# A planned emission order with other costs, one reduction for layer 0's sixteen terms, and a third row-mask buffer in a four-layer graph kernel

## The chip, the core and the metric

The kernel runs on one core of one Trainium2 chip. A core has a matrix engine (TensorE, "PE" in the profile, with its weight load "PEld"), a vector engine (VectorE, "DVE"), a scalar engine (ScalarE, "ACT"), GpSimd ("POOL"), which here only issues transfers, and SyncE ("SP"), which issues the others. Each engine takes its instructions in the order in which the program emitted them, and semaphores let one engine wait for another. The metric is the device time of one launch in microseconds (us), the median of several runs.

## The reference, cut to what matters

There are N = 2048 nodes, a batch of B = 8 and C = 64 features. Each of four layers adds a graph operation to x and normalizes the result over the 64 features.

```
x = layernorm(x + L0(x, adj))
#   L0: As = [I, A, 2*A@A - I];  out[b,n,o] = sum_k sum_i (As[k] @ x)[b,n,i] * w[n,k,i,o] + bias[n,o]
#       w = einsum('nd,dkio->nkio', embedding, weight), d = 16 terms for each node
x = layernorm(x + L1(x, adj))
#   L1: e = leaky_relu(s1[:, :, None] + s2[:, None, :]);  att = softmax(where(adj > 0.5, e, -9e15))
#       elu(att @ x)
x = layernorm(x + L2(x, adj))
#   L2: ((adj + I) @ (x @ W.T + b)) / rowsum(adj + I)
x = layernorm(x + L3(x, adj))
#   L3: three steps of  effects = adj @ v;  v = relu([v, effects] @ W1.T + b1) @ W2.T + b2
```

All data are float32.

## The kernel before, in words

**Tiles.** The eight batches are handled as four pairs (p = 0 to 3); a pair's 2 x 64 features fill 128 columns. `SX[p]` holds the pair's x as 16 tiles of 128 nodes. A product with the adjacency (a "sweep") walks over four column chunks of 512 nodes (c) and eight tiles of 256 x 512 elements (q), which `fetch` loads through SP's queue into a ring of `A_BUFS` buffers of 512 KB (tile `a`). The matmuls of a sweep stand in `sweep` at L1086; they accumulate in PSUM tiles `acc`.

**Layer 0.** `second_pass` (matmuls at L593) makes for each tile of 128 nodes two PSUM tiles `yp`, each with eight of the 16 embedding terms. `add_terms` weights each term with the node's embedding and adds it to `SX`. It has three forms: for most tiles ScalarE writes 16 weighted terms into an `e` buffer (L616) and VectorE adds them pairwise (L630, L632); for pair 0 ScalarE takes the first eight and VectorE adds the others straight to `SX` (L618); and where the plan sees no free `e` buffer, VectorE does all 16. `first_norm` and `layer_norm` (L471 to L498) follow.

**Layer 1.** Row masks (`mr`, L431) are made once from the rows of adj in `row_tile`, and stored in DRAM (`by_row`); column masks (`mk`, L447) likewise (`by_col`). `scores` finds the greatest score of each row: 16 row tiles, each with one mask load (L712) and two VectorE instructions (L724, tile `junk`). `weights` then makes the exponentials column tile by column tile: mask load (L797), VectorE add (L802), ScalarE Prelu (L810), VectorE add (L815), ScalarE Exp (L818), and eight matmuls for two column tiles (L828, tile `po`). Four `e` buffers serve this chain and layer 0's terms. `finish` divides, applies the ELU and normalizes.

**Layers 2 and 3.** After a sweep, `z_evict` or `h_evict` (L946) take the PSUM tile to SBUF, and `tails` runs the small products of a chunk: `ps_emb` (L974), VectorE (L983, L987), the norm, `ps_vT` (transpose, L1008), `ps_u` (L1021), `ps_v` (L1041). Pairs 0 and 1 are done one after the other; pairs 2 and 3 together at the end in `joint_layer2` (L1205) and `joint_layer3` (L1292), which work on sums of quarters of adj that `sums` makes on VectorE (L1165) and stores in DRAM.

**What sets the order.** The program is emitted by a planner. Each piece of work is a Python generator (a "thread") that yields the engine of its next step and the things it waits for. `Plan.go` keeps an estimated time at which each engine is free, picks the thread whose next step could begin earliest, and lets it emit its instructions; `plan.run` advances the engine's estimated time by a cost written in the code. A step on PE counts as ready only `SLACK` us after its inputs are. `Ring` is a set of buffers with estimated times of release. All this happens while the program is built; on the chip only the resulting order per engine and the semaphores remain.

Of the kernel before, what the change touches and what calls it, by code (L numbers as in the profile page):

```python
# [37 lines left out]
class Plan:  # L38
# [6 lines left out]
    SLACK = 2.5  # L45

    def __init__(self):
        self.free = dict.fromkeys(["PE", "DVE", "ACT", "DMA", "SP"], 0.0)
        self.at = {}
        self.threads = []  # L50
        self.count = itertools.count()
# [8 lines left out]
    def run(self, eng, cost, *after):  # L60
        t = max([self.free[eng], *(self.when(a) for a in after)]) + cost
        assert t < NEVER
        self.free[eng] = t
        return t + self.LAG

# [70 lines left out]
def resnorm_d4_kernel(  # L136
# [44 lines left out]
    mr_ring = Ring(wp, "mr", 2)  # L181
# [36 lines left out]
    A_BUFS = 7  # L218
# [7 lines left out]
    def fetch(n):  # L226
        c, q, plus = order_of_a[n]
        t, k = a_ring.take([P, 2, CW], "a")
        freed = a_ring.t
        if isinstance(c, str):  # L230
            src = sum_tiles[c][q]
        else:
            src = a_plus_i[q] if plus and c == q // 2 else tile_of_adj(c, q)
        nc.sync.dma_start(t, src)
        a_tiles[n] = (t, k)
        at["a", n] = plan.run("SP", 1.4, freed) + 3.5
# [23 lines left out]
    blocks = ("w2bd", "w31v", "w31e", "w32bd", "w32c")  # L260
    w2bd, w31v, w31e, w32bd, w32c = (const.tile([P, P], F32, name=n) for n in blocks)
# [107 lines left out]
    def weights_of_l23():  # L369
# [20 lines left out]
        pp_ring.give(k, done)  # L390
        yield "PE", [pp_ring, done]
# [19 lines left out]
    def rows_of_adj():  # L411


        for t in range(NT):
            yield "SP", [115.0 + 9.0 * t, bc_ring]
            an, k = bc_ring.take([P, 2, HALF], "an")
            an = an.rearrange("p a b -> p (a b)")
            nc.sync.dma_start(an, adj[t * P : (t + 1) * P, :])
            done = plan.run("SP", 2.8, bc_ring.t, 115.0 + 9.0 * t) + 9.0
            plan.start(1, row_tile(t, an, k, done))  # L420

    def row_tile(t, an, k, done):
        yield "ACT", [done]
        dg = tiny([P, 1], "dg", 2)
        nc.scalar.activation(an, an, AF.Copy, accum_out=dg)
        done = plan.run("ACT", act(N) + 0.2, done)
        yield "DVE", [done, mr_ring]
        nc.vector.tensor_scalar_add(dg, dg, 1.0)
        nc.vector.reciprocal(rdeg[:, t : t + 1], dg)
        mk, km = mr_ring.take([P, N], "mr", BF16)  # L430
        nc.vector.tensor_scalar(mk, an, THRESHOLD, NEG_INF, ALU.is_le, ALU.mult)  # L431
        done = plan.run("DVE", 1.13 + 0.16, done)
        bc_ring.give(k, done)
        nc.gpsimd.dma_start(by_row[t], mk)
        done = plan.run("DMA", 0.6, done) + 4.0
        mr_ring.give(km, done)
        at["by_row", t] = done + 2.0
        if all(("by_row", i) in at for i in range(NT)):
            at["rows"] = done

    def mask_of_tile(n, t, k):
# [7 lines left out]
        if c == q // 2:  # L449
            yield "DVE", [got]  # L450
            for i in range(2):
                block = t[:, i, (2 * q + i) % TPC * P :][:, 0:P]
                nc.vector.tensor_tensor(block, block, ident, ALU.add)
            got = plan.run("DVE", dve(P, 2), got)
            nc.gpsimd.dma_start(a_plus_i[q], t)
            got = plan.run("DMA", 0.6, got) + 4.0
        a_ring.give(k, max(done, got))
        nc.gpsimd.dma_start(by_col[q][:, :, cols(c)], mk)
        done = plan.run("DMA", 0.8, done) + 4.0
        mk_ring.give(km, done)  # L460
        at["by_col", q, c] = done + 2.0

    def layer_norm(v, n, after, centered=False):
# [4 lines left out]
        if not centered:  # L468
# [7 lines left out]
            done = plan.run("DVE", dve(n, 2) + 0.1, after)  # L476
# [9 lines left out]
        done = plan.run("DVE", dve(n) + 0.1, done)  # L486
# [5 lines left out]
        done = plan.run("ACT", 0.3, done)  # L492
        yield "DVE", [done]

        nc.vector.tensor_tensor(vs, vs, r, ALU.mult)
        nc.vector.scalar_tensor_tensor(vs, vs, -0.5, r, ALU.mult, ALU.mult)
        nc.vector.scalar_tensor_tensor(r, vs, 1.5, r, ALU.add, ALU.mult)
        nc.vector.tensor_tensor(v3, v3, r.unsqueeze(2).to_broadcast([P, nb, C]), ALU.mult)  # L498
        return plan.run("DVE", dve(n) + 0.4, done)
# [7 lines left out]
    def y1_chunk(p, c, pa, ka, done):  # L507
# [6 lines left out]
        stored = plan.run("DMA", 0.6, done) + 3.0  # L514
        at["y1T", p, c] = stored + 2.0
# [23 lines left out]
    def stacks():  # L539

        for n in range(NPAIR * NCH):
# [6 lines left out]
            got = plan.run("DMA", 0.6, xg_ring.t, ("y1T", p, c)) + 4.0  # L548
# [15 lines left out]
    def second_pass():  # L564

        for n in range(NPAIR * NCH):
# [4 lines left out]
            for j in range(TPC):  # L571
                t = c * TPC + j
                cs = slice(j * P, (j + 1) * P)
                for h in range(2):
# [5 lines left out]
                    if h == 0 or ring.ready() > plan.free["PE"]:  # L580
                        yield "PE", [("xg", n + 1), got, ring]
                    if h == 0:


                        terms = None
                        if e_ring.ready() < NEVER:
                            terms = e_ring.take([P, D0, P], "terms")
# [17 lines left out]
    def add_terms(p, c, t, h, yp, ring, k, terms, t_pe, left):  # L605

        shared = p == 0 and terms is not None
        eng = "ACT" if terms and not (shared and h) else "DVE"
        yield eng, [t_pe]
        v = SX[p][:, t, :]  # L610
        for d in range(8):
# [5 lines left out]
            else:  # L617
                nc.vector.scalar_tensor_tensor(  # L618
                    batches(v), term, weight, batches(v), ALU.mult, ALU.add
                )  # L620
        done = plan.run(eng, 8 * (0.25 if eng == "ACT" else 0.265), t_pe)
# [4 lines left out]
        if terms:  # L626
            yield "DVE", [done, ("terms", p, t)]
            for half in (4, 2) if shared else (8, 4, 2):
                a, b = (terms[0][:, i * half : (i + 1) * half, :] for i in range(2))
                nc.vector.tensor_tensor(a, a, b, ALU.add)  # L630
            for d in range(2):
                nc.vector.tensor_tensor(v, v, terms[0][:, d, :], ALU.add)  # L632
            done = plan.run("DVE", 1.4 if shared else 2.5, done, ("terms", p, t))
            e_ring.give(terms[1], done)
# [59 lines left out]
    def scores(p, sv, xc, s_rows, done):  # L694
        s2b = []
        for e in range(2):
# [5 lines left out]
            ready = plan.run("DMA", 0.8, done, bc_ring.t) + 7.5  # L702
# [6 lines left out]
        def load(t):  # L709
# [4 lines left out]
            at["mask", p, t] = plan.run("DMA", 0.6, mr_ring.t, ("by_row", t)) + 5.0  # L714

        plan.start(1, load(0))
        for h in range(2):
            mx = tiny([P, 2, 8], "mx", 4)
            for t in range(8 * h, 8 * h + 8):
                if t + 1 < NT:  # L720
                    plan.start(1, load(t + 1))
# [20 lines left out]
    def greatest(p, h, mx, sv, xc, s_rows, done):  # L742
# [5 lines left out]
        done = plan.run("DVE", 0.16, done)  # L748
# [7 lines left out]
        for name, rows in (  # L756
# [7 lines left out]
            ready = plan.run("DMA", 0.8, done, bc_ring.t) + 8.0  # L764
# [7 lines left out]
    def to_rows(v, rows, done):  # L772
# [12 lines left out]
        done = plan.run("DMA", 0.5, done) + 2.5  # L785
# [5 lines left out]
    def weights(p, h, jt, s1b, mb, sv, po, ready):  # L791
# [6 lines left out]
        got = plan.run("DMA", 0.6, mk_ring.t) + 4.5  # L798
# [14 lines left out]
        done = plan.run("ACT", act(HALF, 2), done)  # L813
# [6 lines left out]
        mine = held.setdefault((p, h), [])  # L820
        mine.append((jt, e, ke, done))
        if jt % 2 == 0:
            return
        yield "PE", [mine[0][3], done, *([("weighed", p, h, jt - 2)] if jt > 1 else [])]
# [14 lines left out]
        mine.clear()  # L839
# [6 lines left out]
    def finish(p, h, po, kpo, xc):  # L846
# [11 lines left out]
        for f in range(2):  # L858
# [24 lines left out]
            done = plan.run("DVE", dve(CW) + 0.12, t_pe)  # L883
# [21 lines left out]
            done = plan.run("DVE", dve(CW, 2) + 0.2, done)  # L905
# [3 lines left out]
        if h == 0:  # L909
            yield "DMA", [("weighted", p, 1)]  # L910
            nc.gpsimd.dma_start(SX[p][:, 0:8, :], stage)
            done = plan.run("DMA", 1.5, *norms) + 3.0
# [57 lines left out]
    def layer2_tail(p, c, z, kz, done):  # L970
# [19 lines left out]
        done = plan.run("DVE", dve(P, TPC) + dve(CW), done)  # L990
# [46 lines left out]
    def last_chunk(p, c, done):  # L1037
# [15 lines left out]
        done = plan.run("DVE", dve(CW, 2), done)  # L1053
# [88 lines left out]
    def pure(k, r):  # L1142
# [3 lines left out]
        for c, q in (quarters(k, r)[i] for i in (0, 3)):  # L1146
            t, kt = xg_ring.take([P, 2, CW], "pure")
            nc.sync.dma_start(t, tile_of_adj(c, q))
            got.append((t, kt, plan.run("SP", 1.4, xg_ring.t) + 4.0))
        return got  # L1150

    def sums(k, r, taken):
# [8 lines left out]
        def out_of(m, a, b, op, *after):  # L1161
# [6 lines left out]
            bc_ring.give(kt, plan.run("DMA", 0.6, done) + 5.0)  # L1168
# [302 lines left out]
```

## Time and profile before

| what | before |
|---|---|
| median of 3 runs | 2172.77 us (2169.68 to 2172.82) |
| the profiled execution | 2177.32 us, its span 2175.5 us |
| mean granted TensorE clock | 0.984 |
| PE busy | 2090.3 us, 96% of the span |
| DVE busy | 1532.3 us, 70% |
| ACT busy | 933.5 us, 43% |
| moved by DMA | 495.85 MB, mean 228 GB/s |
| adjacency tiles, issue to landing | 496 of 512 KB, 5.3 us (median) |
| row-mask loads, issue to landing | 64 of 512 KB, 5.9 us (median) |

The span is the time from the first to the last instruction of one profiled execution; the rest of its time lies around it. "Busy" is the time in which at least one instruction of an engine ran. A line of a group reads: source line, engine, operation, output tile <- input tiles, shapes, count | busy us, mean ns of one | idle us of the engine before them and what ended it. In a table of stretches each engine's busy time is given with its instruction count, then the granted clock (1.00 is full speed), the DMA engines' busy share and the rate in GB/s. An fp32 matmul of the program is two instructions in the profile.

### The profile page before, as it was taken

How to read it: one execution, taken by the hardware profiler on the slowest of the kernel's cores; microseconds unless marked ns; L12 is line 12 of the kernel's file. 1: busy time of each engine (PE TensorE's matmuls, PEld its weight loads, DVE VectorE, ACT ScalarE, POOL GpSimd, SP SyncE). 2: the span in 40 equal slices, each digit the busy share in tenths (PEclk: the TensorE clock that was granted, in tenths of full speed). 3: DMA queues.
4: the chain of work that ended last, by engine and by line, in shares of the span. 5: the costliest groups of instructions: out<-in, count | busy, mean ns of one | idle time of the engine just before them, and what ended most of it. 6: DMA issues, size and time to landing. Idle time of an engine off the chain costs nothing. (4 is left out here: it accounts for less than half of the span.)

```text
span 2175.5 us, 19004 instructions
## 1 busy us (share of the span) xinstructions
PE 2090.3 (96%) x6325; PEld 923.0 (42%) x6325; DVE 1532.3 (70%) x2057; ACT 933.5 (43%) x1605; POOL 213.3 (10%) x374
## 2 busy tenths in 40 slices
PE   8998999999999999999998999989999998999997
PEld 3443444333433333344443444434444454444443
DVE  2226756999799999979998978989797555020214
ACT  0014433476576457767624746417566012000001
POOL 2211001100110110001001011011100110000000
PEclk9999999999999999999999999989999999999999
DMA  9798845633542475446688788778687687878785
GB/s 313 270 328 305 287 133 184 216 107 96 162 150 88 150 234 153 146 126 198 223 289 299 247 286 294 233 249 303 220 293 226 238 301 243 281 251 282 252 291 169
DMA packets 208739, 495.85 MB, mean 228 GB/s; under 512 B 20274, under 2 KB 28594, under 8 KB 204530
## 3 DMA queue, kind: packets, MB, share of 16 engines
q1 hardware_dynamic: 165058, 347.62, 48.3%
q0 software_dynamic: 39360, 144.92, 19.4%
q10 hardware_dynamic: 4224, 2.10, 0.4%
q8 instruction: 50, 0.82, 0.1%
q14 instruction: 47, 0.39, 0.1%
HBM read 446.14 MB, written 46.33 MB: 226 GB/s over the span
## 5 line engine op out<-in xcount | busy, mean ns | idle before, releaser
L1086 PE MATMUL acc<-a,SX 128*128 128x512 f32 x1024 | 470.1, 603 | 9.0 <-DMA SX<-in_x 6.4
L1086 PE MATMUL acc<-a,SA 128*128 128x512 f32 x768 | 352.9, 602 | 8.0 <-ACT SA L348 4.7
L810 ACT ACTIVATE e<-e,sv 128x1024 f32<-128x1024 f32 x256 | 280.4, 1153 | 123.6 <-DVE e L802 117.3
L724 DVE CUSTOM_DVE_ANT_0 junk<-s2b,mr 128x2048 bf16<-128x2048 f32 x128 | 292.7, 2287 | 32.6 <-DMA mr<-by_row 31.3
L818 ACT ACTIVATE e<-e 128x2048 f32<-128x2048 f32 x128 | 245.3, 1925 | 120.5 <-DVE e L815 120.2
L802 DVE TENSOR_TENSOR e<-s1b,mk 128x2048 f32<-128x2048 f32 x128 | 289.6, 2284 | 9.8 <-DMA mk<-by_col 9.8
L815 DVE TENSOR_TENSOR e<-e,mb 128x2048 f32<-128x2048 f32 x128 | 290.2, 2284 | 7.6 <-ACT e L810 7.5
L1086 PEld LDWEIGHTS acc<-a,SX 128*128 128x128 f32 x1024 | 191.7, 193 | 242.7 <-issue 229.1
L593 PE MATMUL yp<-SH,xgT 128*128 128x512 f32 x512 | 250.7, 615 | 1.8 <-DVE SX L618 1.0
L616 ACT ACTIVATE terms<-yp,emb_sb 128x128 f32<-128x128 f32 x768 | 207.9, 396 | 70.9 <-PE yp L593 70.6
L828 PE MATMUL po<-e,SX 128*64 128x512 f32 x1024 | 234.0, 599 | 3.0 <-ACT e L818 3.0
L1086 PEld LDWEIGHTS acc<-a,SA 128*128 128x128 f32 x768 | 142.6, 192 | 182.0 <-issue 168.3
L1292 PE MATMUL acc<-a,t 128*128 128x512 f32 x384 | 169.1, 592 | 0.0
L593 PEld LDWEIGHTS yp<-SH,xgT 128*128 128x128 f32 x512 | 92.4, 193 | 147.6 <-issue 139.0
L593 PE MATMUL yp<-SH,y2T 64*128 64x512 f32 x512 | 134.9, 634 | 17.3 <-ACT terms L616 9.8
L630 DVE TENSOR_TENSOR terms<-terms 128x512 f32<-128x512 f32 (+1 forms) x152 | 111.2, 731 | 35.6 <-ACT terms L616 32.2
L828 PEld LDWEIGHTS po<-e,SX 128*64 128x64 f32 x1024 | 68.0, 137 | 155.6 <-issue 137.8
L797 POOL DMA_DIRECT2D mk<-by_col x128 | 69.3, 542 | 589.4 <-DVE e L802 475.9
L618 DVE SCALAR_TENSOR_TENSOR SX<-yp,emb_sb,SX 128x128 f32<-128x128 f32 x256 | 89.7, 350 | 48.9 <-PE yp L593 40.4
L1086 PE MATMUL acc<-a,SB 128*128 128x512 f32 x256 | 120.1, 601 | 0.0
L1292 PEld LDWEIGHTS acc<-a,t 128*128 128x128 f32 x384 | 72.0, 190 | 86.1 <-issue 86.1
L480 ACT ACTIVATE ln_sq<-SX 128x512 f32<-128x512 f32 x48 | 30.4, 633 | 146.4 <-DVE SX L473 81.1
(226 smaller groups left out, 1704.2 us busy)
## 6 DMA issues: line engine op xcount, KB each, us to landing
a<-in_adj_t SPq DMA_DIRECT2D x496, 512.0 KB, 5.3
a<-s SPq DMA_DIRECT2D x96, 512.0 KB, 4.5
mr<-by_row POOLq DMA_DIRECT2D x64, 512.0 KB, 5.9
mk<-by_col POOLq DMA_DIRECT2D x128, 256.0 KB, 5.6
an<-in_adj SPq DMA_DIRECT2D x16, 1024.0 KB, 9.3
s<-s POOLq DMA_DIRECT2D x32, 512.0 KB, 6.9
a<-a_plus_i SPq DMA_DIRECT2D x24, 512.0 KB, 5.7
by_col<-mk POOLq DMA_DIRECT2D x32, 256.0 KB, 6.1
```

The source lines that it names most:

```text
L593: nc.tensor.matmul(yp[:, e, :], lhsT=y2T[rows, cs] if k2 else xg[:, e, cs], rhs=(wk2 if k2 else w01)[rows, hs], start=(k2 == h), stop=(k2 ...
L616: nc.scalar.activation(batches(terms[0][:, dd, :]), term, AF.Copy, scale=weight)
L618: nc.vector.scalar_tensor_tensor(batches(v), term, weight, batches(v), ALU.mult, ALU.add)
L630: nc.vector.tensor_tensor(a, a, b, ALU.add)
L724: nc.vector.tensor_tensor_reduce(out=junk, in0=s2b[e][0], in1=masks[t][0], scale=1.0, scalar=LOWEST, op0=ALU.add, op1=ALU.max, accum_out=m ...
L802: nc.vector.tensor_tensor(e, s1b[0], mk.unsqueeze(1).to_broadcast([P, 2, HALF]), ALU.add)
L810: nc.scalar.activation(e[:, i, :], e[:, i, :], AF.Prelu, bias=sv[:, 2 + i, jt : jt + 1], alpha=ALPHA)
L815: nc.vector.tensor_tensor(e, e, mb[0], ALU.add)
L818: nc.scalar.activation(e, e, AF.Exp)
L828: nc.tensor.matmul(po[i * C : (i + 1) * C, f, :], lhsT=SX[p][:, t, i * C : (i + 1) * C], rhs=e[:, i, f * CW : (f + 1) * CW], start=(t == 0 ...
L1086: nc.tensor.matmul(pa, lhsT=source[:, m, :], rhs=t[:, i, :], start=(m == 0 and not seed), stop=(m == NT - 1),)
L1292: nc.tensor.matmul(pa, lhsT=B[:, 2 * r + b, :], rhs=at_[:, b, :], start=(r == 0 and b == 0 and not go_on), stop=(r == RQ - 1 and b == 1), ...
```

## The change

The change has these parts. Line numbers below are those of the kernel before.

- The planner: `SLACK` goes from 2.5 to 1.0; a new method `dma` estimates a transfer's end from its size at a shared rate (`RATE` = 340, in KB per us) in place of fixed delays at each call; about a dozen costs of VectorE's and ScalarE's chains become larger, by up to 0.35 us.
- Layer 0: `add_terms` has two forms in place of three. The terms always go to an `e` buffer, for which TensorE's step now waits in the plan. For pair 0 VectorE's eight terms are added in place to ScalarE's eight. The sum of the 16 (or 8) terms is one `tensor_reduce` over an access pattern whose inner step is 128 elements, and one addition to `SX`.
- `layer_norm`: one small VectorE product (L495) is replaced by a Square on ScalarE.
- Buffers: the row-mask ring `mr` has three buffers in place of two and `scores` loads two tiles ahead; `A_BUFS` goes from 7 to 6; the weight block `w32bd` moves into the `stage` buffer; the list `held` of `weights` is keyed by column tile.

The diff, cut to its core:

```diff
-    SLACK = 2.5
+    RATE = 340.0
+    SLACK = 1.0
...
+    def dma(self, queue, kb, *after):
+        t = self.run(queue, 0.4 if queue == "SP" else 0.7, *after) - self.LAG
+        self.moved = max(t + 3.5, self.moved) + kb / self.RATE
+        return self.moved + 0.2
...
-    mr_ring = Ring(wp, "mr", 2)
+    mr_ring = Ring(wp, "mr", 3)
...
-    A_BUFS = 7
+    A_BUFS = 6
...
-        at["a", n] = plan.run("SP", 1.4, freed) + 3.5
+        at["a", n] = plan.dma("SP", 512, freed)
...
-    w2bd, w31v, w31e, w32bd, w32c = (const.tile([P, P], F32, name=n) for n in blocks)
+    w2bd, w31v, w31e, w32c = (const.tile([P, P], F32, name=n) for n in blocks)
+    w32bd_t, w32bd_k = st_ring.take([P, 8, P], "w32bd")
+    w32bd = w32bd_t[:, 0, :]
...
-        done = plan.run("DVE", 1.13 + 0.16, done)
+        done = plan.run("DVE", 1.13 + 0.26, done)
         bc_ring.give(k, done)
         nc.gpsimd.dma_start(by_row[t], mk)
-        done = plan.run("DMA", 0.6, done) + 4.0
+        done = plan.dma("DMA", 512, done)
...
         nc.scalar.activation(r, vs, AF.Ln)
         nc.scalar.activation(r, r, AF.Exp, scale=-0.5)
-        done = plan.run("ACT", 0.3, done)
+        rr = tiny([P, nb], "ln_rr", 2)
+        nc.scalar.activation(rr, r, AF.Square)
+        done = plan.run("ACT", 0.55, done)
         yield "DVE", [done]
-        nc.vector.tensor_tensor(vs, vs, r, ALU.mult)
-        nc.vector.scalar_tensor_tensor(vs, vs, -0.5, r, ALU.mult, ALU.mult)
+        nc.vector.scalar_tensor_tensor(vs, vs, -0.5, rr, ALU.mult, ALU.mult)
...
-                        yield "PE", [("xg", n + 1), got, ring]
+                        yield "PE", [("xg", n + 1), got, ring, *([e_ring] if h == 0 else [])]
                     if h == 0:
-                        terms = None
-                        if e_ring.ready() < NEVER:
-                            terms = e_ring.take([P, D0, P], "terms")
+                        terms = e_ring.take([P, D0, P], "terms")
...
-        shared = p == 0 and terms is not None
-        eng = "ACT" if terms and not (shared and h) else "DVE"
-        yield eng, [t_pe]
+        shared = p == 0
+        eng = "DVE" if shared and h else "ACT"
+        yield eng, [t_pe, *([("terms", p, t)] if shared and h else [])]
...
-                nc.vector.scalar_tensor_tensor(
-                    batches(v), term, weight, batches(v), ALU.mult, ALU.add
-                )
-        done = plan.run(eng, 8 * (0.25 if eng == "ACT" else 0.265), t_pe)
+                to = batches(terms[0][:, d, :])
+                nc.vector.scalar_tensor_tensor(to, term, weight, to, ALU.mult, ALU.add)
+        done = plan.run(eng, 8 * (0.255 if eng == "ACT" else 0.29), t_pe)
...
-            for half in (4, 2) if shared else (8, 4, 2):
-                a, b = (terms[0][:, i * half : (i + 1) * half, :] for i in range(2))
-                nc.vector.tensor_tensor(a, a, b, ALU.add)
-            for d in range(2):
-                nc.vector.tensor_tensor(v, v, terms[0][:, d, :], ALU.add)
-            done = plan.run("DVE", 1.4 if shared else 2.5, done, ("terms", p, t))
+        n = 8 if shared else D0
+        added = tiny([P, P], "added", 1)
+        nc.vector.tensor_reduce(
+            added, terms[0][:, 0:n, :].rearrange("p d n -> p n d"), AX.X, ALU.add
+        )
+        nc.vector.tensor_tensor(v, v, added, ALU.add)
+        done = plan.run("DVE", dve(n * P) + dve(P) + 0.1, done)
...
-            at["mask", p, t] = plan.run("DMA", 0.6, mr_ring.t, ("by_row", t)) + 5.0
+            at["mask", p, t] = plan.dma("DMA", 512, mr_ring.t, ("by_row", t)) + 0.5
         plan.start(1, load(0))
+        plan.start(1, load(1))
...
-                if t + 1 < NT:
-                    plan.start(1, load(t + 1))
+                if t + 2 < NT:
+                    plan.start(1, load(t + 2))
...
-        got = plan.run("DMA", 0.6, mk_ring.t) + 4.5
+        got = plan.dma("DMA", 256, mk_ring.t) + 0.3
...
-        done = plan.run("ACT", act(HALF, 2), done)
+        done = plan.run("ACT", act(HALF, 2) + 0.15, done)
...
-        done = plan.run("DVE", dve(P, TPC) + dve(CW), done)
+        done = plan.run("DVE", dve(P, TPC) + dve(CW) + 0.35, done)
```

## The prediction

> **What bounds the kernel now.** The page's first part and its table of stretches come first: they tell which engine has no idle time, and where it has some.
>
> ```profile
> span 2175.5 us, 19004 instructions
> PE 2090.3 (96%) x6325; PEld 923.0 (42%) x6325; DVE 1532.3 (70%) x2057; ACT 933.5 (43%) x1605; POOL 213.3 (10%) x374
> core 0: us, PE busy (x) PEld busy (x) DVE busy (x) ACT busy (x) POOL busy (x), PEclk, DMA share, GB/s
> 163.00:218.00 55.00, 48.96 (x132) 19.72 (x131) 38.18 (x95) 27.14 (x61) 5.59 (x9) 0.94 0.90 306
> 490.00:544.00 54.00, 53.31 (x165) 19.74 (x165) 52.67 (x66) 36.62 (x50) 3.86 (x7) 1.00 0.32 94
> 1142.00:1197.00 55.00, 47.22 (x129) 20.13 (x128) 46.22 (x36) 23.89 (x25) 9.35 (x17) 0.94 0.84 298
> 1414.00:1469.00 55.00, 44.69 (x126) 21.85 (x124) 45.50 (x71) 8.88 (x22) 6.57 (x12) 0.88 0.72 251
> 1795.00:1850.00 55.00, 46.66 (x161) 26.67 (x160) 29.68 (x61) 11.18 (x25) 4.27 (x8) 0.91 0.74 245
> 1850.00:1904.00 54.00, 54.00 (x139) 24.96 (x138) 4.82 (x7) 2.10 (x3) 0.00 (x0) 1.00 0.83 280
> ```
>
> TensorE bounds the span: 2175.5 - 2090.3 = 85.2 us idle in all. The reader should see where: the last row (pure product work) has none, while four rows lose 6.0, 7.8, 10.3 and 8.3 us, and in those the granted clock is 0.88 to 0.94. VectorE is full (52.67 of 54) in the second row and in most rows from 381 to 1088 us, but TensorE keeps busy beside it with products. So an idle VectorE is no gain by itself; only TensorE's waits are. The waits view says for whom, the timeline what stands behind one:
>
> ```profile
> PE yp L593 <- ACT terms L616: 10.6, 6, 5.7
> PE ps_vT L1008 <- DVE SX L498: 8.3, 2, 6.8
> PE acc L1086 <- DMA a<-in_adj_t: 5.8, 7, 1.7
> PE ps_u L1021 <- ACT SH L946: 5.2, 1, 5.2
> DVE junk L724 <- DMA mr<-by_row: 31.3, 11, 7.9
> 186.58 1.23 DVE L431 TENSOR_SCALAR mr<-an 128x2048 bf16<-128x2048 f32 x1 [10.11 <-DMA by_row<-mr]
> 1163.80 2.29 DVE L724 CUSTOM_DVE_ANT_0 junk<-s2b,mr 128x2048 bf16<-128x2048 f32 x1 [7.86 <-DMA mr<-by_row]
> 1168.34 4.39 ACT L810 ACTIVATE e<-e,sv 128x1024 f32<-128x1024 f32 x4 [22.61 <-DVE e L802]
> 1173.35 2.08 PE L1021 MATMUL ps_u<-ge,SH 128*128 128x128 f32 x8 [5.22 <-ACT SH L946]
> 1430.92 5.79 PE L1086 MATMUL acc<-a,SA 128*128 128x512 f32 x8 [0.68 <-ACT SA L348]
> ```
>
> Read the last lines as a chain: VectorE waits 7.86 us for a row mask, the mask add L802 comes late, ScalarE's Prelu L810 waits for it, the unrelated L946 stands behind that Prelu in ScalarE's queue, and TensorE waits 5.22 us for L946. The final line shows the second price: after a pause eight matmuls take 5.79 us where eight take 3.60 elsewhere (1419.90, same view): half clock.
>
> Sum of what can be won. Of 85.2 us, 6.4 are the wait for the first x (start), 9.8 lie behind the last matmul (2165.7 to the end): 69 us in the middle. The rows with a clock under 1.00 (0.97 five times, 0.94, 0.94, 0.97, 0.88, 0.97, 0.91; last row left out) lose 0.54 of a 54.4 us slice, 29 us, some of it idle already: about 25 us of work time. Together some 94 us; 2175.5 - 94 = 2081.5 us is the floor of this schedule.
>
> **The change, part by part.** Durations are the by-form rows of lines:
>
> ```profile
> L618 DVE SCALAR_TENSOR_TENSOR SX<-yp,emb_sb,SX 128x128 f32<-128x128 f32 x256 | 89.7, 350 | 48.9 <-PE yp L593 40.4
> L630 DVE TENSOR_TENSOR terms<-terms 128x1024 f32<-128x1024 f32 x40 | 48.8, 1219 | 32.3 <-ACT terms L616 32.2
> L630 DVE TENSOR_TENSOR terms<-terms 128x512 f32<-128x512 f32 x56 | 38.6, 689 | 1.4
> L632 DVE TENSOR_TENSOR SX<-SX,terms 128x128 f32<-128x128 f32 x112 | 32.7, 292 | 3.9
> L484 DVE TENSOR_REDUCE ln_v<-ln_sq 128x8 f32<-128x512 f32 x64 | 43.5, 680 | 8.4 <-ACT ln_sq L480 8.3
> L686 DVE COPY xc<-SX 128x32 f32<-128x32 f32 x4 | 0.8, 188 | 0.0
> ```
>
> *Layer 0's sum.* Tiles handled before: 40 by ScalarE terms and a VectorE tree (1219 + 689 + 425 + 2 x 292 = 2.92 us); 16 of pair 0, half each (eight L618 in 3.05 us by the timeline, then 689 + 425 + 584 = 1.70; 4.75); 8 with all 16 terms on VectorE (6.1). After: 48 tiles are one reduction over 2048 elements and one add; 16 tiles are eight terms, one reduction over 1024 and one add. A reduction has no row of this size: from 288 ns for 128 elements (row L375) and 680 for 512 its slope is (680 - 288)/384 = 1.02 ns per element, so 2048 take 2.24 to 2.28 us and 1024 take 1.21 us, if the stride costs nothing. Big tile 2.28 + 0.29 = 2.57; small tile, with terms that no longer wait for each other (L983 issues four such in 1.12 us) 2.25 + 1.21 + 0.29 = 3.75. VectorE saves 40 x 0.35 + 16 x 1.0 + 8 x 3.5 = 58 us.
>
> [...] The reduction reads with 512 bytes between elements. The trace's nearest row is L686: 32 elements 256 bytes apart in 188 ns, against 161 ns for a copy of two elements (L316): 0.9 ns per element, no slower than the reductions' 1.02. By the row the reduction is 2.28 us and VectorE saves 58[...]. I take the row; both ends stay in the range.
>
> The reductions of pair 0 bring a wait: VectorE's eight terms now add into ScalarE's eight and stand behind them, and behind VectorE's stand row masks and xg copies. Bounds: 0, and 16 times ScalarE's 2.18 us, 35 us. Before, VectorE waited 40.4 of 48.9 us at L618 for TensorE's second half, which comes 2.6 us after the first, so ScalarE is normally done: I take 0.
>
> ScalarE gets 128 more terms (207.9/768 = 0.27 us each): +35 us, plus 64 Squares at about 214 ns (row L490): +14. It was 43% busy, 36.62 of 54 us in the fullest kind of row, so other work covers this; uncovered, it delays yp's PSUM release.
> *Layer norm.* L495 goes (64 x 161 = 10.3 us of VectorE); Square adds 0.24 us on ScalarE in the same chain. Path: about zero.
> *No fallback.* A tile of layer 0 now needs one of four e buffers before its matmuls. That is a wait on TensorE's queue; behind it stand all products. Bounds: below zero (no 6.1 us chains), above 8 tiles x one mask-add period of 4.6 us = 37 us, if no buffer were planned for. Nearest row: yp's wait for terms, 10.6 us over 128 tile halves; I take 0.
>
> *w32bd in the stage buffer.* Same memset, same two loads; the stage is first written near 587 us (L902's first start), long after the weights are made: zero, and if that cover were gone one wait of a few us.
>
> *Third row-mask buffer.* In layer 1's first pass the loads run two ahead. VectorE's 31.3 us of waiting (11 times) mostly ends, and the 10.11 us at 186 us, where the stores of three masks blocked it. On TensorE this ended in the stalls of 5.75 us at 202 us (yp for terms, ScalarE held by L480 for VectorE) and 5.22 us at 1173 us. What is late next: mask loads of the second pass (L797), which stand on POOL's queue behind the earlier L712 loads. POOL issues the same 379 instructions.
> *Six adjacency buffers.* One tile of 512 KB lasts 4 x 0.43 = 1.7 us of a single product; one buffer less takes 1.7 us off a lead that must cover a landing of 5.3 us (page, part 6). TensorE waited 5.8 us for these in all. SP's fetches keep their number (677 instructions on SP before and after) but start when a buffer is free. Bounds 0 and 20 us; I take 5.
> *New order.* Counting instructions of both emitted orders with these durations: TensorE has the same work, and 1566 us of it before layer 1's last matmul (before 1561); VectorE has 1403 us before its last mask add (before 1448). So products stay where they were and VectorE has 45 us more room. Against it stands the smaller margin: from ps_emb to its ps_vT the sixteen chunks had 13.7 us of matmuls between them on average, now 10.6, and five of the last eight have 6.0 to 6.2. The chain between (L983 1.12, L987 0.69, L480 0.63, L484 0.68, L485 0.17, three small ScalarE steps 0.66, two VectorE steps 0.40, L498 0.69) is 5.0 us without hand-overs and without VectorE's other queue.
>
> Gain by stretch, idle and half clock together: 163 to 218 us, 8 of 9 (mask buffer). 218 to 979, 13 of 27 (shorter chains; half). 1034 to 1197, 12 of 16 (the 5.2 us stall with its clock, half of the rest). 1306 to 1469, 14 of 21 (products waited for chunks between score passes). 1686 to 1850, 4 of 18 (the thin margin is here). Sum 51. Less 5 for the buffers and 4 for thinner margins elsewhere: 42. Span 2175.5 - 42 = 2133.5. The profiled run took 2177.3; the median shown is 2172.8, 2.7 below the span: 2131.
>
> **The rivals.** *Stalls return.* TensorE had 46 waits in its list. If 1.5 us less margin lengthens each by 0.75, 35 us and about 10 of half clock cancel the gain: 2172. For: 6.0 us against a 5.0 us bare chain. Against: the planned chain costs were raised by up to 0.35 us.
> *The stride costs double (slower).* VectorE +59 us, mostly from 300 to 945 us, where it has about 25 us free; 35 reach TensorE, 10 more by half clock, against about 20 of gain elsewhere: 2198. It decides from 58/114,688 = 0.5 ns extra per element. L686 speaks against it.
> *Transfers bind.* Each of some 600 fetches 0.06 us late gives 36 us: 2167. Against: in rows with a DMA share of 0.83 TensorE has no idle time.
> *More is won.* If nearly all middle stalls go: 2090.
>
> **How the numbers follow.** Forecast 0.55 (2131, own range 2105 to 2155); more 0.10; stalls return 0.22 (2150 to 2195); stride 0.08; transfers 0.05. A measurement of this kernel can tell about 0.2%, 4 us. Faster: 0.55 + 0.10 + 0.08 + 0.02 = 0.75; same 0.06 + 0.01 = 0.07; slower 0.08 + 0.08 + 0.02 = 0.18. Range 2092 to 2186: it leaves out half of "more", most of "stride", the ends of the others.
>
> **What would show it.** Right: added<-terms at 2.3 us; VectorE near 1470 us busy; junk's wait for mr under 10 us; no stall over 4 us near 200 and 1170 us; TensorE idle near 50 us, mean clock 0.99. Wrong: the reduction over 3 us; ps_vT or ps_u waiting for L510 or L954 (L498 and L946 now) at more than 15 us; waits for in_adj_t over 15 us; more rows with a clock under 1.00 than now.

## The result, and the profile after

| | before | after |
|---|---|---|
| median | 2172.77 us (2168.69 to 2175.51, 9 runs) | 2166.04 us (2163.59 to 2170.27, 9 runs) |
| profiled span, mean granted clock | 2175.5 us, 0.984 | 2164.4 us, 0.991 |

The ratio is 0.9974, 95% interval [0.9963, 0.9984]: 6.7 us faster, where 42 were forecast (2131 us). In the page of the changed kernel the line of engines comes first, then the same stretches as before (TensorE's idle time is the second number less the third):

```profile
span 2164.4 us, 18851 instructions
PE 2081.7 (96%) x6325; PEld 917.0 (42%) x6325; DVE 1552.5 (72%) x1727; ACT 977.9 (45%) x1799; POOL 213.6 (10%) x374
core 0: us, PE busy (x) PEld busy (x) DVE busy (x) ACT busy (x) POOL busy (x), PEclk, DMA share, GB/s
163.00:218.00 55.00, 55.00 (x162) 23.55 (x159) 41.57 (x98) 29.08 (x70) 4.99 (x9) 1.00 0.98 346
381.00:435.00 54.00, 47.88 (x125) 19.98 (x125) 53.62 (x41) 23.44 (x68) 9.41 (x17) 0.94 0.65 214
1142.00:1197.00 55.00, 50.67 (x143) 22.60 (x142) 54.59 (x56) 21.87 (x27) 8.77 (x16) 1.00 0.98 360
1414.00:1469.00 55.00, 50.63 (x156) 25.01 (x155) 53.49 (x65) 8.51 (x19) 8.19 (x15) 1.00 0.93 335
```

TensorE still idles 82.7 us (2164.4 - 2081.7; before 85.2). Of the 11.1 us by which the profiled span fell, 8.6 are shorter busy time (2090.3 to 2081.7) at the higher mean clock. The three stretches that were picked out for their waits did improve: the one at 163 us lost 6.0 us and loses none now, at 1142 us 7.8 became 4.3, at 1414 us 10.3 became 4.4, all three at full clock. But VectorE, which was to fall by 58 us to about 1474, rose from 1532.3 to 1552.5. The groups by form (each shape of an instruction on its own line) and the waits of VectorE and TensorE show where:

```profile
L636 DVE TENSOR_REDUCE added<-terms 128x128 f32<-128x2048 f32 x48 | 177.3, 3694 | 47.5 <-ACT terms L624 47.5
L636 DVE TENSOR_REDUCE added<-terms 128x128 f32<-128x1024 f32 x16 | 30.7, 1916 | 0.2
DVE junk L732 <- DMA mr<-by_row: 0.5, 1, 0.5
PE ps_xg L564 <- ACT terms L624: 7.0, 2, 4.2
PE ps_rows L785 <- DVE mx L755: 6.6, 2, 4.7
PE yp L601 <- ACT y2T L543: 6.1, 1, 6.1
PE ps_vT L1016 <- DVE SX L510: 5.1, 5, 1.6
```

The reduction takes 3.69 us in place of the assumed 2.28, and 1.92 in place of 1.21. VectorE's wait for the row mask is gone (31.3 us before). In TensorE's list `ps_xg` waits 7.0 us for `terms` (2.2 before) and `yp` 6.1 us for `y2T` (2.1 before), and the wait of `ps_rows` for `mx` is new; these three lie between 428 and 880 us, where layer 0's sums and layer 1's scores share VectorE. The wait of `yp` for `terms`, the largest before, fell from 10.6 to 3.9 us. Taken as one stretch (order: before, after):

```profile
218.00:979.00 761.00, 740.48 (x2239) 302.70 (x2238) 661.48 (x928) 444.39 (x968) 73.16 (x132) 0.99 0.49 159
218.00:979.00 761.00, 726.75 (x2190) 297.18 (x2188) 664.09 (x636) 455.34 (x1065) 74.47 (x135) 0.98 0.48 160
```

Its idle time rose from 20.5 to 34.3 us, where 13 us of gain had been forecast. One stall of it in the timeline, in order of time:

```profile
414.44 3.66 DVE L636 TENSOR_REDUCE added<-terms 128x128 f32<-128x2048 f32 x1
418.34 2.28 DVE L732 CUSTOM_DVE_ANT_0 junk<-s2b,mr 128x2048 bf16<-128x2048 f32 x1
423.37 6.70 DVE L810 TENSOR_TENSOR e<-s1b,mk 128x2048 f32<-128x2048 f32 x3
425.75 2.19 ACT L818 ACTIVATE e<-e,sv 128x1024 f32<-128x1024 f32 x2 [19.22 <-DVE e L810]
427.96 0.59 ACT L543 COPY y2T<-acc 128x512 f32<-128x512 f32 x1
428.60 3.66 PE L601 MATMUL yp<-SH,y2T 64*128 64x512 f32 x8 [6.12 <-ACT y2T L543]
```

VectorE is a queue without gaps here (53.62 of 54 us). The mask add L810 comes late behind the reductions; ScalarE has waited 19.22 us for it with its Prelu L818; the eviction L543, which needs nothing from VectorE, stands behind that Prelu; TensorE waits 6.12 us for L543 and then takes 3.66 us for eight matmuls that take 1.99 us in *inner* below; the granted clock from 428.6 to 432.3 us is 0.54. It is the chain of the old stall at 1173 us in a new place: a late VectorE blocks ScalarE, which blocks a copy that TensorE needs.

### The profile page after: what moved, and what is told of

The parts are those of the page before. It is cut to its first block, busy times and chain, and to the rows that moved or that the text cites. A ratio compares the mean times of both kernels' runs of the same rounds, so it can differ in the third digit from the quotient of the medians.

```text
span 2164.4 us, 18851 instructions
## 1 busy us (share of the span) xinstructions
PE 2081.7 (96%) x6325; PEld 917.0 (42%) x6325; DVE 1552.5 (72%) x1727; ACT 977.9 (45%) x1799; POOL 213.6 (10%) x374
## 4 chain that ended last, share of the span: by engine, by line
PE 40%; DVE 26%; issue 25%; ACT 5%; DMA 3%; POOL 1%; POOLq 0%; ACTq 0%; SPq 0%; DVEq 0%
PE acc L1094 26%; DVE added L636 8%; PE po L837 6%; DVE junk L732 5%; DVE e L810 5%; PE yp L601 5%; DVE e L823 4%; ACT terms L624 2%; DMA a<-in_adj_t 2%; ACT e L818 1%; PE ps_u L1029 1%; PE acc L1083 1%; POOL s L1175 1%; ACT e L826 1%; DVE ln_v L495 1%
## 5 line engine op out<-in xcount | busy, mean ns | idle before, releaser
L818 ACT ACTIVATE e<-e,sv 128x1024 f32<-128x1024 f32 x256 | 279.5, 1147 | 162.8 <-DVE e L810 161.6
L810 DVE TENSOR_TENSOR e<-s1b,mk 128x2048 f32<-128x2048 f32 x128 | 289.3, 2283 | 0.9 <-DMA mk<-by_col 0.6
L624 ACT ACTIVATE terms<-yp,emb_sb 128x128 f32<-128x128 f32 x896 | 242.2, 394 | 78.5 <-PE yp L601 78.3
L636 DVE TENSOR_REDUCE added<-terms 128x128 f32<-128x2048 f32 (+1 forms) x64 | 208.0, 3249 | 47.7 <-ACT terms L624 47.5
L601 PEld LDWEIGHTS yp<-SH,y2T 64*128 64x128 f32 x512 | 43.7, 188 | 88.3 <-issue 73.4
## 6 DMA issues: line engine op xcount, KB each, us to landing
an<-in_adj SPq DMA_DIRECT2D x16, 1024.0 KB, 10.6
```

The costliest lines, as they stand in the source:

```text
L601: nc.tensor.matmul(yp[:, e, :], lhsT=y2T[rows, cs] if k2 else xg[:, e, cs], rhs=(wk2 if k2 else w01)[rows, hs], start=(k2 == h), stop=(k2 ...
L624: nc.scalar.activation(batches(terms[0][:, dd, :]), term, AF.Copy, scale=weight)
L636: nc.vector.tensor_reduce(added, terms[0][:, 0:n, :].rearrange("p d n -> p n d"), AX.X, ALU.add)
L810: nc.vector.tensor_tensor(e, s1b[0], mk.unsqueeze(1).to_broadcast([P, 2, HALF]), ALU.add)
L818: nc.scalar.activation(e[:, i, :], e[:, i, :], AF.Prelu, bias=sv[:, 2 + i, jt : jt + 1], alpha=ALPHA)
```

## The experiments

Four theories are tried: the stride of the reduction costs VectorE time that reaches TensorE; the thinner margin brings the stalls back; the new plan goes wrong because it priced the reduction and its addition at 2.5 us; the buffers give or take something by themselves.

### The same additions without the stride

*tree*: the changed kernel with contiguous additions; the plan, and so the order, is the same.

```diff
-        nc.vector.tensor_reduce(
-            added, terms[0][:, 0:n, :].rearrange("p d n -> p n d"), AX.X, ALU.add
-        )
-        nc.vector.tensor_tensor(v, v, added, ALU.add)
+        for half in (4, 2) if shared else (8, 4, 2):
+            a, b = (terms[0][:, i * half : (i + 1) * half, :] for i in range(2))
+            nc.vector.tensor_tensor(a, a, b, ALU.add)
+        for d in range(2):
+            nc.vector.tensor_tensor(v, v, terms[0][:, d, :], ALU.add)
```

> The changed kernel with the emission order it has, but each tile's terms are summed by the old chain of contiguous additions in place of the one reduction. Theory 1 (the reduction's 512-byte inner step makes it 3.69 us where 2.28 were assumed, and layer 0's TensorE stalls follow from that): VectorE's busy time falls from 1552 us by about 48 x (3.69 + 0.29 - 2.65) + 16 x (1.92 + 0.29 - 1.70) = 72 us, TensorE's idle time between 218 and 1030 us falls by 15 to 25 us, and the time goes from 2166 to 2135-2150. Theory 2 (the smaller margin SLACK makes the stalls, VectorE's time is hidden): VectorE falls alike, the time stays within 5 us of 2166.

Measured: 2127.29 us, ratio to before 0.9793 [0.977, 0.9815]: 39 us less than the changed kernel, where 16 to 31 were expected.

```profile
PE 2070.8 (97%) x6325; PEld 915.6 (43%) x6325; DVE 1494.4 (70%) x1903; ACT 979.0 (46%) x1799; POOL 214.0 (10%) x374
218.00:979.00 761.00, 753.15 (x2297) 309.64 (x2297) 650.48 (x835) 488.41 (x1146) 76.30 (x138) 1.00 0.50 165
```

VectorE's busy time fell by 58 us, not by 72, since the tree of a big tile takes 2.92 us and not the 2.65 of the expectation. TensorE's idle time in the stretch fell from 34.3 to 7.9 us.

*inner*: the changed kernel with the 16 terms innermost in the buffer, so that the same one reduction reads 16 adjacent values, and ScalarE and VectorE write theirs 64 bytes apart. Again the same plan and order.

```diff
-                        terms = e_ring.take([P, D0, P], "terms")
+                        terms = e_ring.take([P, P, D0], "terms")
...
-                nc.scalar.activation(batches(terms[0][:, dd, :]), term, AF.Copy, scale=weight)
+                nc.scalar.activation(batches(terms[0][:, :, dd]), term, AF.Copy, scale=weight)
...
-                to = batches(terms[0][:, d, :])
+                to = batches(terms[0][:, :, d])
...
-            added, terms[0][:, 0:n, :].rearrange("p d n -> p n d"), AX.X, ALU.add
+            added, terms[0][:, :, 0:n], AX.X, ALU.add
```

> The changed kernel with the terms stored with the sixteen terms innermost: the reduction reads contiguously, ScalarE (and VectorE for pair 0) writes with a step of 64 bytes. Theory 1: the reduction takes 2.28 and 1.21 us, VectorE's busy time falls by 48 x 1.41 + 16 x 0.70 = 79 us, the time goes to 2130-2150, less well if ScalarE's strided writes become slower than 0.27 us each. Theory 2: the time stays within 5 us of 2166.

Measured: 2121.48 us, ratio 0.9762 [0.9741, 0.9783], the fastest version of all, and again below the expected range. From the page of *inner*, its groups by form and its stretches:

```profile
PE 2068.0 (98%) x6325; PEld 915.8 (43%) x6325; DVE 1485.9 (70%) x1727; ACT 984.7 (47%) x1799; POOL 214.0 (10%) x374
L636 DVE TENSOR_REDUCE added<-terms 128x128 f32<-128x2048 f32 x48 | 109.5, 2281 | 52.9 <-ACT terms L624 51.4 <-ACT ln_r L501 1.3
L636 DVE TENSOR_REDUCE added<-terms 128x128 f32<-128x1024 f32 x16 | 19.4, 1214 | 0.2
L627 DVE SCALAR_TENSOR_TENSOR terms<-yp,emb_sb,terms 128x128 f32<-128x128 f32 x128 | 45.2, 439 | 46.5 <-PE yp L601 46.4
218.00:979.00 761.00, 757.99 (x2314) 312.71 (x2313) 646.14 (x687) 500.33 (x1162) 76.73 (x139) 1.00 0.51 166
```

Without the stride the reductions take 2281 and 1214 ns, as the prediction assumed (2.28 and 1.21 us). The stride therefore costs 48 x 1.413 + 16 x 0.702 = 79 us of VectorE's time, 0.69 ns for each of 114,688 elements. VectorE's own terms L627, now read and written 64 bytes apart, give 12 us of it back (128 x 96 ns, 439 against 343 in the changed kernel), and the busy times differ by 1552.5 - 1485.9 = 66.6 us, as 79 - 12 would have it. The 58 us that the prediction wanted to save come out too: 1532.3 - 1485.9 = 46 us, and the 12 us of L627. On the path the gain is 45 us (2166.0 - 2121.5). The stretch from 218 to 979 us idles 3.0 us in place of 34.3 and its clock is 1.00 in place of 0.98; TensorE gets through 2314 instructions there in place of 2190. Most of the 45 us are won there. The mask add and ScalarE's eviction of the stall shown above come 11 us earlier in *inner*:

```profile
412.35 6.87 DVE L810 TENSOR_TENSOR e<-s1b,mk 128x2048 f32<-128x2048 f32 x3 [0.63 <-DMA mk<-by_col]
414.74 2.19 ACT L818 ACTIVATE e<-e,sv 128x1024 f32<-128x1024 f32 x2 [10.80 <-DVE e L810]
416.95 0.59 ACT L543 COPY y2T<-acc 128x512 f32<-128x512 f32 x1
```

### The strided reduction alone

*s_only*: the kernel before with the reduction in place of its tree (the reverse of the diff of *tree*), with the old plan, the old order and the old row masks. To make room for the tile `added`, `w32bd` moves into the `stage` buffer here as in the change.

> The kernel before with the strided reduction alone in place of the tree of additions; plan's costs and buffers as before. Theory 1 (the reduction's stride costs about 1.4 us on the big tile and 0.7 on the small one, and this lies on the path): VectorE's busy time rises to about 1550 us, and the time to 2185 to 2205 us. Theory 2 (VectorE has slack enough, the extra is hidden): 2172 within 5, with VectorE as busy. If the reduction alone gave a gain, under 2165, the cause lies elsewhere.

Measured: 2209.43 us, ratio 1.0182 [1.0166, 1.0199], somewhat above the expected 2185 to 2205.

```profile
PE 2096.8 (95%) x6325; PEld 923.9 (42%) x6325; DVE 1582.6 (72%) x1905; ACT 934.4 (42%) x1605; POOL 213.8 (10%) x374
L633 DVE TENSOR_REDUCE added<-terms 128x128 f32<-128x2048 f32 x40 | 147.6, 3691 | 30.5 <-ACT terms L619 30.4
L633 DVE TENSOR_REDUCE added<-terms 128x128 f32<-128x1024 f32 x16 | 30.6, 1914 | 0.0
218.00:979.00 761.00, 718.29 (x2137) 290.60 (x2133) 679.51 (x774) 427.27 (x928) 73.19 (x132) 0.98 0.47 154
```

A big tile costs 3.69 + 0.29 = 3.98 us against 2.92 for the tree, a small one 1.91 + 0.29 = 2.21 against 1.70: 40 x 1.06 + 16 x 0.51 = 50.6 us, and VectorE's busy time is 50.3 us up. Of these, 39 us reach the end (2209.4 - 2170.5, the kernel before in the same set of runs). So by itself this part makes the kernel slower by about as much as the rest makes it faster.

### The stride measured by itself

*probe* has no layers; VectorE and ScalarE run single instructions with different steps between fp32 elements. It was run once; the durations are means of four.

```diff
+STEPS = {"a": 1, "b": 2, "c": 4, "d": 8, "e": 16, "f": 32, "g": 64, "h": 128}
...
+                nc.vector.tensor_reduce(t, src[k], AX.X, ALU.add)
...
+                nc.vector.tensor_copy(t, src[k])
...
+                ("suma", T[:, 0:2048].rearrange("p (n d) -> p n d", d=16)),
+                ("sumb", T[:, 0:2048].rearrange("p (d n) -> p n d", n=128)),
+                ("sumd", T[:, 0:2112].rearrange("p (d n) -> p n d", n=132)[:, 0:128, :]),
```

> Nothing of the layers is computed: only VectorE and ScalarE instructions with different steps between elements, the output is zeros. If a step beyond 16 bytes costs the same at any size, reductions of 256 elements go from 0.42 us at steps of 1 and 2 elements to about 0.6 us (1.74 ns per element) at all steps of 4 or more, and the kernel's own 128 sums of 16 take 1.74 ns per element whatever the padding. If only steps that are a multiple of some larger size are slow (a conflict), the patterns padded to 129, 132 or 136 elements are at 1.04 ns per element. A copy of 32 elements at 256 bytes takes 0.19 us as in the kernel; if a copy of 256 at that step takes 0.6 us, the short copy misled by its fixed part.

Its groups by form; the letter behind the name is the step (a = 1 element, b = 2, c = 4, g = 64), `sumb` has the kernel's own pattern, `sumd` rows of 132:

```profile
L29 DVE TENSOR_REDUCE reda<-T 128x1 f32<-128x256 f32 x4 | 1.6, 405 | 3.2 <-ACT T L54 3.2
L29 DVE TENSOR_REDUCE redb<-T 128x1 f32<-128x256 f32 x4 | 1.6, 408 | 0.0
L29 DVE TENSOR_REDUCE redc<-T 128x1 f32<-128x256 f32 x4 | 2.4, 591 | 0.0
L29 DVE TENSOR_REDUCE redg<-T 128x1 f32<-128x256 f32 x4 | 2.3, 571 | 0.0
L32 DVE COPY cpya<-T 128x256 f32<-128x256 f32 x4 | 1.1, 285 | 0.0
L32 DVE COPY cpyc<-T 128x256 f32<-128x256 f32 x4 | 1.5, 381 | 0.0
L32 DVE COPY cpyg<-T 128x256 f32<-128x256 f32 x4 | 1.8, 443 | 0.0
L37 DVE COPY shortg<-T 128x32 f32<-128x32 f32 x4 | 0.8, 200 | 0.0
L47 DVE TENSOR_REDUCE suma<-T 128x128 f32<-128x2048 f32 x4 | 9.2, 2294 | 0.0
L47 DVE TENSOR_REDUCE sumb<-T 128x128 f32<-128x2048 f32 x4 | 14.3, 3578 | 0.1
L47 DVE TENSOR_REDUCE sumd<-T 128x128 f32<-128x2048 f32 x4 | 15.0, 3749 | 0.1
```

For a reduction a step of two elements (8 bytes) is free (408 ns against 405). The whole price is due at four elements (16 bytes, 591 ns), and 256 bytes cost no more (571); a copy pays 96 ns more at 16 bytes and 158 at 256. Rows of 132 elements do not help (3749 ns against 3578), so the price does not come from the distance of 512 bytes in particular. The doubling that the prediction's rival supposed, an estimate of its author, is not reached: over the whole instruction the factor is 1.4 to 1.5 for the 256 elements of `red` and 1.56 for `sumb`. The copies show how the row L686 misled. A contiguous copy of 256 takes 285 ns; against the 161 ns for two elements that the prediction quoted, this is (285 - 161)/254 = 0.49 ns per element. The strided ones take (443 - 200)/224 = 1.08 between 32 and 256. So L686's 0.9 belongs to a slowed copy, not to an unslowed one. (The expectation's 0.6 us for the strided copy of 256 was too much; that it would mislead beside the reductions was right.)

### The price in the plan

*planned*: the changed kernel, its reduction kept, with the reduction's true cost in the plan.

```diff
-        done = plan.run("DVE", dve(n * P) + dve(P) + 0.1, done)
+        done = plan.run("DVE", 0.00174 * n * P + dve(P) + 0.27, done)
```

> The changed kernel with the reduction as it is, but the planner is given its measured time (0.00174 us per element, so 4.0 us for a tile in place of 2.5): only the order changes. Theory 3 (not the time itself but the plan's wrong price causes the stalls): TensorE's idle time between 218 and 1030 us falls by half, the time goes to 2140-2150. Theory 1: VectorE is as busy as before (1552), the order helps a little, 2155-2165. Theory 2: 2166.

Measured: 2165.62 us, ratio 0.9978 [0.9968, 0.9988].

```profile
218.00:979.00 761.00, 749.20 (x2243) 307.84 (x2242) 673.38 (x656) 465.76 (x1085) 70.89 (x128) 0.99 0.50 163
1034.00:1197.00 163.00, 139.45 (x471) 64.68 (x470) 151.35 (x163) 76.41 (x90) 16.29 (x30) 0.96 0.69 241
```

One sign of theory 3 came true: from 218 to 1030 us TensorE's idle time halved, from 35.7 to 18.3 us, so the stalls of layer 0 do depend on the price in the plan. But they were not saved, only moved. From 1034 to 1197 us 23.6 us are idle in place of 6.8 (the largest wait is now 8.3 us, at 1059 us), and the sum stays (2167.5 - 2083.5 = 84.0 us; 82.7 in the changed kernel). So the correct price alone buys nothing in the order that came of it. It is one order, though, and below it will be seen how much an order is worth; the stride's cost is measured by the variants that keep an order: *tree*, *inner* and *s_only*.

### The buffers

*m_only*: the kernel before with three row masks, six adjacency buffers, loads two ahead (and `w32bd` in the `stage` buffer, to make room); its plan's costs and margin, and its tree, kept. The order changes.

```diff
-    mr_ring = Ring(wp, "mr", 2)
+    mr_ring = Ring(wp, "mr", 3)
...
-    A_BUFS = 7
+    A_BUFS = 6
...
         plan.start(1, load(0))
+        plan.start(1, load(1))
...
-                if t + 1 < NT:
-                    plan.start(1, load(t + 1))
+                if t + 2 < NT:
+                    plan.start(1, load(t + 2))
```

> The kernel before with the buffers alone changed: three row-mask buffers, six adjacency buffers, the masks loaded two graphs ahead (w32bd moved into the stage buffer to make the room); the plan's costs and layer 0's sum stay as they were. Theory A (the third mask buffer is worth a real gain by itself, through the waits of junk for mr near 200 and 1170 us and part of the one near 1440): 2145 to 2160 us, with the wait of junk for mr falling from 31 us to under 3. Theory B (the wait for the mask only stands where another wait would stand): 2172 within 4. Theory C (six adjacency buffers cost more than the mask buffer brings): over 2176, with acc waiting for in_adj_t above 10 us.

Measured: 2158.28 us, ratio 0.9943 [0.9927, 0.9959], 12 us faster than the kernel before in the same set of runs. Its stretches and waits:

```profile
163.00:218.00 55.00, 55.00 (x158) 23.43 (x155) 39.62 (x100) 28.91 (x62) 6.28 (x9) 1.00 0.94 335
1034.00:1197.00 163.00, 154.59 (x493) 69.06 (x494) 157.17 (x162) 74.50 (x82) 18.92 (x35) 0.99 0.83 289
DVE junk L728 <- DMA mr<-by_row: 1.6, 1, 1.6
PE acc L1090 <- DMA a<-in_adj_t: 13.1, 11, 2.1
```

The row-mask wait goes from 31.3 to 1.6 us and the stretch at 163 us loses its 6.0 us of idle, as the prediction had it; from 1034 to 1197 idle falls from 12.9 to 8.4 us. The price is there as well: `acc` waits 13.1 us for adjacency tiles, and 4.5 us more at L1209, where it was 5.8 in all before. The third buffer is not the only way to end the row-mask waits: *plan_only* below, with two buffers in the new plan, has 1.8 us of them.

*inner_mr2*: *inner* with these buffer edits undone.

> The inner kernel with two row-mask buffers, seven adjacency buffers and loads one graph ahead, as before the change. If the third mask buffer matters in the new order too, 2132 to 2148 us with junk's wait for mr back above 15 us; if it doesn't, 2121 within 4.

Measured: 2152.24 us, ratio 0.992 [0.9906, 0.9933]: 31 us slower than *inner*, a little beyond the expected range, but not by the wait that the expectation named, for the waits read:

```profile
DVE junk L731 <- DMA mr<-by_row: 4.0, 3, 2.4
PE po L836 <- ACT e L825: 11.8, 3, 6.7
PE ps_vT L1015 <- DVE v L1007: 5.8, 1, 5.8
```

With two buffers the planner places the loads, and with them everything else, differently, and stalls appear at other places (6.7 us at 971, 5.8 at 1083). The edit changes the row masks, the adjacency buffers, the loads and the order at once, so it is not shown that the third buffer is worth 31 us.

### The margin and the plan

*inner_slack*, *inner_s14* and *inner_s07* are *inner* with other margins; *slack_only* is the kernel before with the new margin; *plan_only* is the changed kernel with the tree of *tree* and the buffers of *inner_mr2*. For the margins one diff is shown; in the others its numbers differ.

```diff
-    SLACK = 1.0
+    SLACK = 2.5
```

> The inner kernel with the planner's margin SLACK at 2.5 in place of 1.0. If the thinner margin of the change costs time (as one rival of the prediction had it), 2110 to 2117 us; if the thinner margin brings time, 2125 to 2135; if it is worth nothing, 2121 within 3.

> The kernel before with the margin SLACK at 1.0 in place of 2.5 and nothing else. If the plan's gain is the margin's, about -28 as in the inner kernel: 2140 to 2148 us. If the thin margin pays only with measured costs behind it, since the old costs err by more than it covers: 2168 us or more, up to 2185.

> The changed kernel with the old buffers (two row masks, seven adjacency buffers, loads one graph ahead) and the old tree of additions: what is left of the change is the plan (its costs, the modelled transfers, the margin of 1.0) and the Square on ScalarE. If the three parts simply add (buffers alone -12, reduction alone +39, all three -4), the plan is worth -31: 2138 to 2142 us. If the plan needs the third buffer to be worth anything (with it the reordered kernel lost 31 where the kernel before gained 12), 2155 to 2172 us, with junk's wait for mr above 15 us.

> The inner kernel with the margin at 0.7 in place of 1.0. If time goes on falling with the margin (28 us from 2.5 to 1.0, some 19 us for each unit), 2114 to 2118 us; if below 1.0 the waits come back, 2125 or more; if flat, 2121 within 3.

> The inner kernel with the margin at 1.4. On a straight line between the two measured (2121 at 1.0, 2149 at 2.5), 2127 to 2131 us. If the 28 us are not a slope but the luck of one order against another, anything from 2118 to 2150.

| kernel | margin | us | ratio to before |
|---|---|---|---|
| *inner_s07* | 0.7 | 2130.57 | 0.9805 [0.9785, 0.9824] |
| *inner* | 1.0 | 2121.48 | 0.9762 [0.9741, 0.9783] |
| *inner_s14* | 1.4 | 2154.59 | 0.992 [0.9903, 0.9938] |
| *inner_slack* | 2.5 | 2149.32 | 0.9899 [0.9885, 0.9913] |
| *slack_only* (before) | 1.0 | 2158.94 | 0.9945 [0.9926, 0.9964] |
| *plan_only* | 1.0 | 2163.26 | 0.996 [0.9946, 0.9973] |

No run shows the thin margin to cost time: at 2.5 *inner* is 28 us slower (4 to 14 were expected), and the kernel before gains 14 us from 1.0 alone, which met neither of its two expectations. But it is no slope either. At 1.4 the time is no better than at 2.5 and above both expected ranges, and 0.7 is worse than 1.0: each value deals another order, and such orders lie up to 33 us apart. *plan_only* missed its first expectation by some 23 us and met the second in time alone, since its wait of `junk` for `mr` is 1.8 us: the buffers alone bring 12 us, the plan alone 10, both (*tree*) 44. Whether that is a true joint effect, or the luck of one order, these runs cannot tell, since one order's scatter is as large as what would have to be explained.

## Why the prediction was wrong

**The step that failed** is the length of the reduction: "By the row the reduction is 2.28 us and VectorE saves 58 [...] I take the row". It put the cost of the stride at nothing. The reductions measured 3.69 and 1.92 us, the stride cost 79 us of VectorE's time, and in place of the 58 us saved its busy time rose by 20. TensorE felt it: removing the stride in the same order gave 39 us (*tree*) and 45 us (*inner*), and adding it to the kernel before cost 39 us (*s_only*). The row L686, on which this rested, was read wrongly: a copy's rate was held against a reduction's rate, and the copy had no contiguous partner beside it. With the duration that was assumed (*inner*) the kernel takes 2121 us, and with the old additions (*tree*) 2127, both inside the forecast's own range of 2105 to 2155. In *inner* TensorE idles 47.7 us (2115.7 - 2068.0), as the prediction had it among its signs of being right (near 50). So the rest of the sum came out near the forecast as a whole. With orders 33 us apart this may be luck in part, and it does not show that each part is worth what was forecast.

**By stretch**, TensorE's idle time (before; after; *inner*; in the late stretches *inner* is some 45 us ahead, so its work there is not quite the same): 163 to 218: 6.0; 0; 0.2, forecast as won and won. 218 to 979: 20.5; 34.3; 3.0, the forecast's 13 us became a loss of 14 with the stride, and are there without it. 1034 to 1197: 12.9; 6.8; 4.2, of the 12 us 6 are there in the changed kernel, and at most 3 more by the clock (0.98 to 1.00 over 163 us). 1306 to 1469: 12.9; 4.4; 4.4, 8.5 us and up to 8 by the clock (0.95 to 1.00), for 14. 1686 to 1850: 11.8; 11.0; 7.2, of the 4 us 0.8 in idle time and up to 3 by the clock (0.96 to 0.98). What the prediction calls half clock is not quite that: its eight matmuls of 5.79 us take 1.6 times the 3.60, and the granted clock over them (1430.9 to 1436.7 us, before) is 0.63, 0.50 only from 1431 to 1433; in the 5.9 us before them (1425 to 1430.9) TensorE idled 3.0 us, at a granted clock of 0.78.

**The waits that were costed at nothing** stayed near it. VectorE's eight terms L627 waited for TensorE alone (46.2 us, the second half of the tile), never for ScalarE's eight, and the 16 reductions of pair 0 for 0.2 us. In the changed kernel's waits no engine waits for L636 or L639, which free the `e` buffers, so the dropped fallback cost nothing that the trace shows. `ps_vT` waited 5.1 us in all for L510 (8.3 for L498 before), so the thin margins were cheap there, and TensorE's two waits for `in_adj_t` are 10.5 and 2.9 us where 5.8 stood: 7.6 us more, forecast 5.

**The rivals.** "The stride costs double" supposed, as an estimate, another 1.02 ns for each of 114,688 elements: 117 us, less the 58 saved, is its 59. It had the cause and, nearly, the size on the path: 0.69 ns extra per element, beyond its deciding point of 0.5, and 39 us (*s_only*, *tree*) to 45 us (*inner*) on the path for its 45. It ended at 2198 because it gave the rest of the change 20 us; the rest was worth 44 (*tree* against before). Its chance of 0.08 rested on the row L686; as no row of before showed a reduction with a large step, that was the wrong weight. "Stalls return" came near the measured time (2172 for 2166) by another cause: stalls did come, but with the stride gone and the same thin margin (*inner*) they are not there. "Transfers bind" has the DMA share of 0.98 from 1142 to 1197 us and three waits of 1.0 to 1.7 us for adjacency tiles there, a few us in all. Nothing came of "more is won" (2090): the fastest variant takes 2121 us.

## What to carry to other kernels

A row of the trace speaks for a strided pattern only beside the same operation without the stride; where there is none, one instruction with and without the stride should be measured before the rest (here 3578 against 2294 ns). Replacing several contiguous instructions with one strided one can lose more than it saves: here 1.06 us on a 2.92 us tile; putting the summed index innermost kept the single instruction and took 45 us off, while the writers paid 12 us of VectorE's busy time and 14 us of ScalarE's (L624, 242.2 to 256.4). Where an order comes from a planner, a change of one constant deals a new order, so an effect below that scatter (33 us here) is only shown by variants that keep the order, as *tree*, *inner* and *s_only* do. What *m_only*, *plan_only* and *slack_only* gain (10 to 14 us) lies below it.

## What was not expected of the hardware

The price of a stride for a reduction is a step and not a slope at the distances measured: 405 and 408 ns at 4 and 8 bytes, 591 at 16, 571 at 256 (a sum of 256). It is due on writes too. In *probe* one copy of 512 elements from PSUM is written contiguously, then with 64 and with 256 bytes between elements (the tile's line of each engine: shortest, median, longest in ns):

```profile
L53 DVE COPY T<-pm x12: 691/1011/1012, 63.1 to 164.5; 128x512 f32<-128x512 f32 x12
L54 ACT COPY T<-pm x12: 586/1012/1013, 63.8 to 165.5; 128x512 f32<-128x512 f32 x12
```

The shortest is the contiguous one, and both strided ones take the rest: on ScalarE a factor of 1.73. In *inner* ScalarE paid this price 896 times at 128 elements: one of its L624 lasts 494 ns in place of 394. But they overlap (eight take 2.29 us in place of 2.18), and its whole busy time grew by only 984.7 - 977.9 = 6.8 us over the changed kernel's.
